# Layer 3 on one core: one run of local attention over all four images, with the other images' norms, projections and experts as steps beside it

## The chip, the core and the metric

One core of one Trainium2 chip runs the whole program in one launch. The metric is device microseconds of one execution, the median of the runs of a measurement; lower is better. The engines of the core that the profile names are PE (matmul; its weight loads are PEld), DVE (vector), ACT (scalar), POOL (GpSimd) and SP, whose queue issues every DMA of the part that is changed.

## What is computed

The program is a chain of four hybrid layers over a batch of 4 images of 64x64 tokens with 128 channels, all in float32. Layers 0 to 2 (a selective scan, a gated recurrence, an attention and a sparse expert layer) are not touched and are left out here. Layer 3 takes the tokens `t` (4 images x 4096 tokens x 128) and computes a local attention and then a mixture of 8 experts, each on a layer norm and each added back:

```python
t = t + _L3_attn_ref(_ln_t(t), ...)
t = t + _L3_ffn_ref(_ln_t(t), ...)

# _L3_attn_ref
xb = x @ w_down.T + b_down                      # 128 -> 16 channels
win = transpose(xb[:, idx, :])                  # windows of 144 tokens, every 72
q, k, v = split(win.reshape(-1, 144, 16) @ in_proj_w.T + in_proj_b, 3)
attn = softmax(q @ k.T / 2)                     # 4 heads of 4 channels, 144 x 144 a window
o = (attn @ v) @ out_proj_w.T + out_proj_b
att = overlap_add(o) / counts
out = x + sigmoid(gate) * (att @ w_up.T + b_up)
return layer_norm(out) * ln_gamma + ln_beta

# _L3_ffn_ref
router_probs = softmax(x @ router_w + router_b)         # 8 experts
top_p, top_i = top_k(router_probs, 2); top_p /= top_p.sum(-1)
expert_out = einsum('bnd,edc->bnec', x, expert_w) + expert_b
return einsum('bnk,bnkc->bnc', top_p, take(expert_out, top_i))
```

An image has 56 windows. Four of them are worked on together, one on each group of 32 rows of the PE, so an image is 14 "turns" of the attention (`NM` = 14).

## The kernel before

`layer3` works image by image. `windows(b)` and `chosen(b)` are Python generators: each `yield` gives the word back to the loop that drives them, and what stands between two yields is a step. The order of PE's instructions is exactly the order in which the steps are recorded (`manual_schedule(engines={PE})`); the order of the other engines and of SP's queue is decided by the framework when the program is built, by data and buffers, and is then fixed too. Every engine takes its instructions in that order, so an instruction that waits holds up all behind it on its engine.

`windows(b)` has these parts. They are named here as the text uses them.

- **Norms and down-projection** ("front"). All 8 blocks of 512 tokens are loaded into one tile `t` that stays for the whole image. A block is normalised (`cm.layer_norm`, L135 to L142: statistics on DVE, a square root on ACT, a reciprocal and four multiply-subtracts on DVE), transposed by PE (L103), copied out of PSUM by ACT (L105) and projected to 16 channels (L1727, sum with the bias L1731).
- **Projections.** The 16-channel tokens go to DRAM and come back as windows in `f` (the text's "wait for f"). Then, for 3 turns at a time, PE makes `kt` (L1771), the queries `qm` of four heads (L1775) and the values `vt` (L1785); ACT and DVE copy them out of the PSUM buffers `mm`, of which there are two.
- **Attention.** For each turn: `largest` (L1807: scores, reduced to row maxima by DVE, L1815) runs 4 turns ahead; `turned` (L1825) transposes the maxima and sends them through DRAM into `qm`; `weights` (L1847: scores again, exponentials on ACT, L1854), `values` (L1870, into the PSUM tile `po`, copied by ACT, L1881) and `divided` (L1889; DVE L1894, L1895). Half a turn is two `weights`, two `values`, one `largest` and one `divided`. `largest` and `weights` each take both buffers of the PSUM pool `s`.
- **Recombination and up-projection** ("back"). The halves of the windows are added (`rec`), transposed (L1945), projected up (L1962), added to the tokens (DVE, L1967), normalised, scaled and shifted (three POOL instructions of 128x512 each, L1970 to L1976).

`chosen(b)` does the expert part of an image: a norm and transpose for each block (L103, L142), the router (L1989), softmax and the two best of 8 on DVE ("gating"), and then, for each block, a transposition of the gate weights (L2040), the bias of the experts (L2048), and for each 128 tokens two matmuls of four experts each (L2058), every one of which is followed by four DVE instructions (L2064) that add the four experts' outputs with their weights to the tokens. These 64 matmuls of an image are called "expert matmuls". Each writes the PSUM pool `x`, which has one buffer, so one matmul cannot begin until the four DVE instructions of the one before are done.

The loop that drives them makes one step of `chosen(b - 1)` at each yield of `windows(b)`, that is four a turn, and ends what is left before the next image:

```python
for b in range(B):
    for _ in windows(b):
        next(before, None)
    for _ in before:
        pass
    before = chosen(b)
for _ in before:
    pass
```

So image 0's attention stands alone, those of images 1 to 3 have the expert matmuls of the image before among them, norms, projections and recombination stand between the attentions, and the experts of image 3 stand alone at the end.

Of the kernel before, what the change touches and what calls it, by code (L numbers as in the profile page):

```python
# [14 lines left out]
P = 128  # L15
# [1588 lines left out]
def layer3(cm, W, M, cst, x2, out):  # L1604
# [6 lines left out]
    with ExitStack() as ctx:  # L1611
# [4 lines left out]
        tp = ctx.enter_context(tc.tile_pool(name="ct", bufs=2))  # L1616
        ep = ctx.enter_context(tc.tile_pool(name="ce", bufs=10))
# [75 lines left out]
        for i in range(2):  # L1693
            vp = tl(wp, [HALF, 2, G, NH, 32], f"vp{i}")
            nc.gpsimd.memset(vp, 0.0)
            vps.append(vp)

# [11 lines left out]
        def windows(b):  # L1709

            t = tl(tp, [P, NT, D], "t")
            kept[b] = t
            for k in range(NBLK):
                nc.sync.dma_start(
                    t[:, 4 * k : 4 * k + 4, :],
                    x2[b, k * BLK : (k + 1) * BLK, :].rearrange("(t p) c -> p t c", p=P),
                )
            xl = tl(bp, [P, NT, D], "xl")
            xb = tl(bp, [P, NT, DK], "xb")
            xb_d = tl(dr, [S, DK], "xb_d")  # L1720
            xTs = {}

            def down(k):
                xT = xTs.pop(k)
                ps = tl(pp, [P, 4, DK], "mm")
                for i in range(4):
                    nc.tensor.matmul(  # L1727
                        ps[:, i, :], lhsT=xT[:, i * P : (i + 1) * P], rhs=wdT,
                        start=True, stop=True,
                    )  # L1730
                nc.vector.tensor_tensor(  # L1731
                    xb[:, 4 * k : 4 * k + 4, :], ps,
                    bdn.unsqueeze(1).to_broadcast([P, 4, DK]), ALU.add,
                )

            for k in range(NBLK):
                part = xl[:, 4 * k : 4 * k + 4, :]
                cm.layer_norm(part, t[:, 4 * k : 4 * k + 4, :], p2)
                xT = tl(p2, [P, BLK], "xT")
                cm.transpose4(xT, part, pp, "mm", act=True)  # L1740
                xTs[k] = xT
                yield
                if k:
                    down(k - 1)
            down(NBLK - 1)
# [17 lines left out]
            qm = tl(bp, [P, NM, NH, WIN], "qm")  # L1763
            kt = tl(bp, [P, NM, WIN], "kt")
            vt = tl(bp, [HALF, NM, 2, G, NH, HD + 1], "vt")
            for m0 in range(0, NM, GW):
# [3 lines left out]
                ps = tl(pp, [P, GW, WIN], "mm")  # L1770
                nc.tensor.matmul(ps[:, 0:g], lhsT=wk4, rhs=f[:, ms, :], start=True, stop=True)  # L1771
                nc.scalar.copy(kt[:, ms, :], ps[:, 0:g])
                for h in range(NH):
                    ps = tl(pp, [P, GW, WIN], "mm")
                    nc.tensor.matmul(  # L1775
                        ps[:, 0:g], lhsT=wq4[:, h, :], rhs=fq, start=True, stop=True
                    )
                    if h % 2:
                        nc.scalar.copy(qm[:, ms, h, :], ps[:, 0:g])
                    else:  # L1780
                        nc.vector.tensor_copy(qm[:, ms, h, :], ps[:, 0:g])
                ps = tl(pp, [HALF, GW, 2, G * NH * (HD + 1)], "mm")
# [6 lines left out]
                nc.vector.tensor_copy(  # L1789
# [3 lines left out]
                yield  # L1793

            mxs = {}

            def largest(m, a):
                if m % 2 == 0 and a == 0:  # L1800
                    mxs[m // 2] = tl(p2, [QC, G, 2, 2 * QN], "mx")
                mx = mxs[m // 2]
                ss = [tl(sp, [P, 2, BLK], "s") for _ in range(2)]
                for r in range(QN):
                    for i in range(G):
                        rows = slice(32 * i, 32 * i + 32)
                        nc.tensor.matmul(  # L1807
                            ss[i // 2][0:QC, i % 2, r * WIN : (r + 1) * WIN],
                            lhsT=qm[rows, m, 2 * a : 2 * a + 2, :].rearrange(
                                "p h q -> p (h q)"  # L1810
                            )[:, r * QC : (r + 1) * QC],
                            rhs=kt[rows, m, :], start=True, stop=True,
                        )
                for p in range(2):
                    nc.vector.tensor_reduce(  # L1815
                        mx[:, 2 * p : 2 * p + 2, m % 2, a * QN : (a + 1) * QN],
                        ss[p][0:QC, :, 0 : QN * WIN].rearrange("p j (r k) -> p j r k", k=WIN),
                        AX.X, ALU.max, negate=True,
                    )

            def turned(m):
                mx = mxs.pop(m // 2)
                n = G * 2 * 2 * QN
                ps = tl(pp, [P, BLK], "mm")
                nc.tensor.transpose(  # L1825
                    ps[0:n, 0:QC], mx.rearrange("p i m x -> p (i m x)"), cm.ident[0:QC, 0:QC]
                )
                mT = tl(p2, [n, QC], "mT")
                nc.vector.tensor_copy(mT, ps[0:n, 0:QC])
                m_d = tl(dr, [G, 2 * NH * WIN], "m_d")  # L1830
                nc.sync.dma_start(m_d.rearrange("i (x q) -> (i x) q", q=QC), mT)
                for i in range(G):
                    nc.sync.dma_start(
                        qm[32 * i + DK : 32 * i + R, m - 1 : m + 1].rearrange(
                            "p m h q -> p (m h q)"
                        ),
                        m_d[i : i + 1, :],
                    )

            o = tl(bp, [HALF, NM, G, 2, DK], "o")  # L1840
            es, oxs = {}, {}

            def weights(m, c, a):
                ss = [tl(sp, [P, 2, BLK], "s") for _ in range(2)]
                for i in range(G):
                    rows = slice(32 * i, 32 * i + 32)
                    nc.tensor.matmul(  # L1847
                        ss[i // 2][0:HALF, i % 2, 0 : 2 * WIN],
                        lhsT=kt[rows, m, c * HALF : (c + 1) * HALF],
                        rhs=qm[rows, m, 2 * a : 2 * a + 2, :], start=True, stop=True,  # L1850
                    )
                for p in range(2):
                    e = tl(ep, [HALF, 2, 2, WIN], "e")
                    nc.scalar.activation(  # L1854
                        e.rearrange("p j h q -> p j (h q)"), ss[p][0:HALF, :, 0 : 2 * WIN],
                        AF.Exp, scale=0.5,
                    )
                    es[m, p, c, a] = e

            def values(m, i):  # L1860
                p, j = divmod(i, 2)
                vp = vps[m % 2]
                if i == 0:
                    nc.gpsimd.tensor_copy(  # L1864
                        vp[:, :, :, :, 0 : HD + 1].rearrange("p c i h d -> p (c i h) d"),
                        vt[:, m].rearrange("p c i h d -> p (c i h) d"),
                    )
                for c in range(2):
                    for h in range(NH):
                        nc.tensor.matmul(  # L1870
                            po[32 * h : 32 * h + 32, j, :],
                            lhsT=vp[:, c, i, h, :], rhs=es[m, p, c, h // 2][:, j, h % 2, :],
                            start=(c == 0), stop=(c == 1),
                        )
                if j == 0:
                    return
                for c in range(2):
                    for a in range(2):
                        del es[m, p, c, a]
                ox = tl(p2, [P, 2, WIN], "ox")  # L1880
                nc.scalar.copy(ox, po)  # L1881
                oxs[m, p] = ox

            def divided(m, p):
                ox = oxs.pop((m, p))
                pt = tl(pp, [P, 4, NH, 32], "mm")
                for j in range(2):
                    for c in range(2):
                        nc.tensor.transpose(  # L1889
                            pt[0:HALF, 2 * j + c].rearrange("p h d -> p (h d)"),  # L1890
                            ox[:, j, c * HALF : (c + 1) * HALF], cm.ident,
                        )
                rc = tl(p2, [HALF, 4, NH], "rc")
                nc.vector.reciprocal(rc, pt[0:HALF, :, :, HD])  # L1894
                nc.vector.tensor_tensor(  # L1895
                    o[:, m, 2 * p : 2 * p + 2].rearrange("p j c (h d) -> p (j c) h d", d=HD),
                    pt[0:HALF, :, :, 0:HD],
                    rc.unsqueeze(3).to_broadcast([HALF, 4, NH, HD]), ALU.mult,
                )

            AHEAD = 4
            for m in range(-AHEAD, NM + 2):
                for x in range(4):
                    if 0 < m <= NM:
# [269 lines left out]
```

## Time and profile before

| | us |
|---|---|
| time before, median of 3 runs | 11145.42 (11142.15 to 11153.18) |
| the profiled execution, time | 11161.64 |
| its span, first to last instruction | 11159.9 |
| last matmul of layer 2 ends, at | 9152.9 |
| first `largest` of images 0, 1, 2, 3, at | 9267.2, 9692.8, 10120.5, 10551.6 |
| last `divided` of image 3 ends, at | 10806.6 |

Of the span, layers 0 to 2 take the first 9153 us and layer 3 the last 2007. Busy shares over the whole span are PE 85%, DVE 69%, POOL 49% and ACT 47%, but they mix the layers: POOL works almost only in layer 0. The profile's rows name engine, line, operation, output and inputs; PEclk is the clock that the throttle granted to PE, 1.00 being full speed. A float32 matmul of this kernel shows as two records, so "x2" on a row of one matmul is one matmul.

### The profile page before, as it was taken

The page shows a single profiled execution, that of the slowest core. Times are in us where ns is not written, and L with a number is a line of the kernel's source. Part 1 is how long each engine was busy: PE and PEld are TensorE (multiplying, and loading weights), DVE is VectorE, ACT ScalarE, POOL GpSimd, SP SyncE. Part 2 cuts the span into 40 slices and gives each one's busy share as a digit, 9 for nine tenths or more (in the row PEclk, how much of TensorE's full clock was granted, in tenths as well). Part 3 has the DMA queues.
Part 4 walks back from the last instruction along what each step waited for, and adds up shares of the span by engine and source line. Part 5 has one row for each costly group of instructions (what it writes and reads, how often), then busy time and mean ns, then how long its engine had stood idle before and what let it go on. Part 6 is the DMA issues. An engine that isn't in the chain of part 4 may idle for free. (4 is left out here: it accounts for less than half of the span.)

```text
span 11159.9 us, 163057 instructions
## 1 busy us (share of the span) xinstructions
PE 9472.5 (85%) x59368; PEld 4541.5 (41%) x59368; DVE 7705.4 (69%) x11365; ACT 5228.1 (47%) x13128; POOL 5468.6 (49%) x2661
## 2 busy tenths in 40 slices
PE   6889998889998899988899946999999858678685
PEld 2344443344443344443344423444444344344442
DVE  1899998888998888888899965635450132565563
ACT  6666544555445564445542124767776512132230
POOL 0778888878888888888899920000000000110110
PEclk7899999889998899998899968999999965688785
DMA  5334443334443334433333241111100180000100
GB/s 145 107 104 151 138 125 118 112 106 154 137 125 124 115 119 148 135 123 116 104 111 100 92 128 37 39 30 41 33 22 16 54 221 5 6 15 10 15 8 8
DMA packets 1378486, 975.88 MB, mean 87 GB/s; under 512 B 694980, under 2 KB 1195432, under 8 KB 1373336
## 3 DMA queue, kind: packets, MB, share of 16 engines
q1 hardware_dynamic: 1377688, 965.45, 28.9%
q8 instruction: 475, 7.78, 0.3%
q14 instruction: 323, 2.65, 0.1%
HBM read 650.24 MB, written 314.83 MB: 86 GB/s over the span
## 5 line engine op out<-in xcount | busy, mean ns | idle before, releaser
L657 DVE TENSOR_TENSOR_SCAN big<-dA,db 128x1024 f32<-128x1024 f32 x2048 | 4679.7, 2286 | 81.1 <-ACT dA L564 2.8
L673 POOL TENSOR_TENSOR big<-big,ct 128x2048 f32<-128x2048 f32 x1024 | 4645.5, 4537 | 84.7 <-DVE big L657 5.7
L641 PE MATMUL db<-dg,du 64*64 64x512 f32 x16384 | 2449.2, 619 | 100.5 <-DVE db L654 87.6
L686 PE MATMUL aux<-big,both 128*64 128x256 f32 x16384 | 2116.1, 402 | 465.2 <-DVE db L654 258.4
L686 PEld LDWEIGHTS aux<-big,both 128*64 128x64 f32 x16384 | 1205.0, 142 | 1462.9 <-issue 628.0
L705 ACT COPY yr<-aux 128x64 f32<-128x64 f32 x1024 | 226.6, 222 | 2759.4 <-PE aux L686 1295.4
L641 PEld LDWEIGHTS db<-dg,du 64*64 64x64 f32 x16384 | 747.3, 136 | 1328.7 <-issue 1224.6
L612 ACT ACTIVATE dg<-mask,BT 128x64 f32<-128x64 f32 x4096 | 1007.3, 341 | 4.4 <-DMA dg_d<-dg 4.4
L1443 PE MATMUL av<-e,x 128*128 128x512 f32 x2048 | 974.0, 592 | 4.6 <-ACT e L1438 4.6
L1394 PE MATMUL qk<-a,xT 128*128 128x512 f32 x2048 | 966.6, 594 | 8.6 <-ACT e L1398 7.8
L1398 ACT ACTIVATE e<-qk,nk 128x512 f32<-128x512 f32 x1024 | 692.9, 685 | 540.1 <-PE qk L1394 539.2
L564 ACT ACTIVATE dA<-dp,A 128x252 f32<-128x252 f32 x2048 | 870.7, 509 | 1.4
L973 POOL TENSOR_TENSOR g_rs<-g_rs,qrow 128x4 f32<-128x4 f32 x32 | 41.1, 1285 | 1500.4 <-DVE g_rs L972 1500.4
L1864 POOL COPY vp<-vt 72x160 f32<-72x160 f32 x56 | 18.9, 343 | 1470.8 <-PE po L1870 1074.9
L665 POOL TENSOR_TENSOR cy<-big,a 128x32 f32<-128x32 f32 x1008 | 269.3, 267 | 764.2 <-DVE big L657 483.8
L1394 PEld LDWEIGHTS qk<-a,xT 128*128 128x128 f32 x2048 | 378.0, 190 | 462.4 <-issue 358.0
L2064 DVE SCALAR_TENSOR_TENSOR t<-x,gw,t 128x128 f32<-128x128 f32 x1024 | 354.1, 346 | 301.5 <-PE x L2058 278.4
L1443 PEld LDWEIGHTS av<-e,x 128*128 128x128 f32 x2048 | 381.6, 190 | 434.7 <-issue 393.7
L1438 ACT ACTIVATE e<-e 128x1024 f32<-128x1024 f32 x510 | 538.7, 1056 | 15.3
L654 DVE TENSOR_TENSOR db<-db,cy 128x16 f32<-128x16 f32 x2016 | 336.5, 167 | 268.8 <-PE db L641 220.2
L2058 PE MATMUL x<-ew,x3T 128*128 128x512 f32 x512 | 365.0, 802 | 158.6 <-DVE t L2064 153.6
L1854 ACT ACTIVATE e<-s 72x576 f32<-72x576 f32 x448 | 269.3, 642 | 475.9 <-PE s L1847 475.4
(491 smaller groups left out, 10720.8 us busy)
## 6 DMA issues: line engine op xcount, KB each, us to landing
ct<-ct_d SPq DMA_DIRECT2D x1024, 128.0 KB
dg_d<-dg SPq DMA_DIRECT2D x256, 512.0 KB
dg<-dg_d SPq DMA_DIRECT2D x256, 512.0 KB
xo<-xT_d SPq DMA_DIRECT2D x2048, 32.0 KB
x<-xc_d SPq DMA_DIRECT2D x144, 264.0 KB
dp<-dl_d SPq DMA_DIRECT2D x256, 128.0 KB
t2k<-in_x SPq DMA_DIRECT2D x96, 256.0 KB
sp<-sp_d SPq DMA_DIRECT2D x16, 1280.0 KB
```

The lines of the kernel that those rows point to most:

```text
L564: nc.scalar.activation(w["dA"][:, :, g, n, 1:], w["dp"][:, g, :, 1:], AF.Exp, scale=A[:, w["h"], g, n : n + 1],)
L612: nc.scalar.activation(q["dg"][:, n, :], mask, AF.Copy, scale=BT[:, q["c"], n : n + 1])
L641: nc.tensor.matmul(bs[j][p * TC : (p + 1) * TC, g * NH0 : (g + 1) * NH0, :], lhsT=q["du"][kp][half, g * TC : (g + 1) * TC], rhs=q["dg"][ha ...
L657: nc.vector.tensor_tensor_scan(st[:, u].rearrange("p n t -> p (n t)"), q["w"]["dA"][:, c % QC].rearrange("p g n t -> p (g n t)"), bs[j].re ...
L673: nc.gpsimd.tensor_tensor(sv, sv, q["ct"].rearrange("p n t -> p (n t)").unsqueeze(1) .to_broadcast([P, 4, NH0 * TC]), ALU.mult,)
L686: nc.tensor.matmul(yp[p * TC : (p + 1) * TC], lhsT=both, rhs=st[:, :, p * NH0 + n, :], start=(n == 0), stop=(n == NH0 - 1 and not late),)
L1394: nc.tensor.matmul(ps, lhsT=me["xT"][:, kt * P : (kt + 1) * P], rhs=me["a"][k], start=True, stop=True,)
L1398: nc.scalar.activation(e[:, j, :], ps, AF.Exp, bias=me["nk"][:, kt : kt + 1], scale=2.0)
L1438: nc.scalar.activation(es[g + 2], es[g + 2], AF.Exp)
L1443: nc.tensor.matmul(avs[b, k], lhsT=img[b]["x"][:, kt, :], rhs=e[:, j, :], start=(kt == 0), stop=(kt == NT - 1),)
L2058: nc.tensor.matmul(s.rearrange("p e c -> p (e c)"), lhsT=x3T[:, j * P : (j + 1) * P], rhs=ew[:, 4 * a : 4 * a + 4, :].rearrange("p e c -> ...
L2064: nc.vector.scalar_tensor_tensor(t[:, j, :], s[:, e, :], gw[:, j, 4 * a + e : 4 * a + e + 1], t[:, j, :], ALU.mult, ALU.add,)
```

## The change

Layer 3 is rewritten around one loop over all 56 turns of the four images.

- `largest`, `turned`, `weights`, `values` and `divided` count turns `T` from 0 to 55 through all images. There are two sets of `qm`, `kt` and `vt` (a pool `qp` of two buffers), so the maxima of an image's first turns can be made while the image before is still in its last ones.
- `windows` is split: `front(b)` (norms, down-projection, projections), `merged(b)` (the additions of `rec`) and `back(b)` (recombination, up-projection, norm). `front(0)` runs first, alone. The others are put on a list `todo` with `chosen(b)`, and `step()` does the next step of the first entry. The loop calls `step()` 13 times in half a turn (6 times in an even quarter, 7 in an odd one).
- Beside image 0's attention stands `front(1)`; from the end of image b on, beside the attention of image b+1, stand `back(b)`, then `front(b + 2)`, then `chosen(b)`. After the last turn come `back(3)` and `chosen(3)`, alone.
- Matmuls of the steps beside the attention write the one buffer of the pool `x` (`own_bank`): transposes, projections, router, biases and experts alike. Where nothing runs beside (`front(0)`, `back(3)`, `chosen(3)`), they use the two buffers of `s` (`free_bank`).
- Tokens are kept in DRAM, not in a tile: blocks of 512 tokens come in two buffers `tin`; the normalised ones (`xl`) and the attention's result (`t`) are written to DRAM and loaded again. `chosen` does an image in two halves of 4 blocks and loads its tokens twice.
- A norm takes its root on POOL (a power of -0.5 on 128x4), and the scaling is done by four ACT instructions instead of four on DVE. The three POOL instructions of 128x512 in `back` go to DVE; the copies of `qm` and `vt` that DVE made go to ACT.

A step count for each part follows from the yields: `back` 56, `front` 125 (49 for the norms, 16 empty ones for the way through DRAM, 60 for the projections), `chosen` 228 (two halves of 24 for the norms, 10 for the gating and 80 for the experts). The 14 turns of an image have 364.

```diff
+        qp = ctx.enter_context(tc.tile_pool(name="cq", bufs=2))
...
+        mroot = tl(wp, [P, 1], "mroot")
+        nc.vector.memset(mroot, -0.5)
...
+        def own_bank():
+            return tl(xp, [P, BLK], "x")
+
+        def free_bank():
+            return tl(sp, [P, 2, BLK], "s")[:, 0, :]
+
+        def block(a, b, k, tag="tin"):
+            t = tl(tp, [P, 4, D], tag)
+            nc.sync.dma_start(t, rows(a, b, k))
+            return t
...
+            nc.vector.tensor_scalar(rs[:, 0, :], mv[:, :, 1], 1e-5, None, ALU.add)
+            nc.gpsimd.tensor_tensor(
+                rs[:, 0, :], rs[:, 0, :], mroot.to_broadcast([P, 4]), ALU.pow
+            )
+            nc.vector.scalar_tensor_tensor(
+                rs[:, 1, :], mv[:, :, 0], -1.0, rs[:, 0, :], ALU.mult, ALU.mult
+            )
...
+        def normalise(dst, src, rs):
+            for i in range(4):
+                nc.scalar.activation(
+                    dst[:, i, :], src[:, i, :], AF.Identity,
+                    bias=rs[:, 1, i : i + 1], scale=rs[:, 0, i : i + 1],
+                )
...
+                ps = bank()
+                turned4(ps, xl)
+                xT = tl(p2, [P, BLK], "xT")
+                nc.scalar.copy(xT, ps)
+                yield
+                yield
+                ps = bank()[:, 0 : 4 * DK].rearrange("p (i d) -> p i d", d=DK)
...
-                nc.gpsimd.tensor_tensor(
-                    dst, dst, gam.unsqueeze(1).to_broadcast([P, 4, D]), ALU.mult
-                )
...
+                nc.vector.tensor_tensor(
+                    xl, xl, gam.unsqueeze(1).to_broadcast([P, 4, D]), ALU.mult
+                )
+                nc.vector.tensor_tensor(t, t, bet.unsqueeze(1).to_broadcast([P, 4, D]), ALU.add)
+                yield
+                nc.vector.tensor_tensor(t, t, xl, ALU.add)
+                nc.sync.dma_start(rows(me["t"], 0, k), t)
...
-                        s = tl(xp, [P, 4, D], "x")
+                        s = bank()
                         nc.tensor.matmul(
...
                         yield
+                        yield
...
+            for _ in front(0, free_bank):
+                pass
+            fronts = {1: front(1, own_bank)}
+            todo.append(fronts[1])
+            for T in range(-AHEAD, LAST + 2):
+                b, m = divmod(T + AHEAD, NM)
+                if m == 0 and 0 < b < B:
+                    while fronts[b] in todo:
+                        step()
+                for x in range(4):
+                    if 0 < T <= LAST:
+                        values(T - 1, x)
+                    step()
+                    if x % 2 == 0 and T + AHEAD < LAST:
+                        largest(T + AHEAD, x // 2)
+                    if x == 2 and T % 2 == 0 and 1 < T + AHEAD <= LAST:
+                        turned(T + AHEAD - 1)
+                    step()
+                    step()
+                    if x == 2 and 0 < T <= LAST:
+                        divided(T - 1, 0)
+                    step()
+                    if x == 0 and 1 < T:
+                        divided(T - 2, 1)
+                        b, m = divmod(T - 1, NM)
+                        if m == 0:
+                            merged(b - 1)
+                            todo.append(back(b - 1, own_bank if b < B else free_bank))
+                            if b + 1 < B:
+                                fronts[b + 1] = front(b + 1, own_bank)
+                                todo.append(fronts[b + 1])
+                            if b < B:
+                                todo.append(chosen(b - 1, own_bank))
+                    step()
+                    if 0 <= T < LAST:
+                        weights(T, x // 2, x % 2)
+                    step()
+                    if x % 2:
+                        step()
+            while todo:
+                step()
+            for _ in chosen(B - 1, free_bank):
+                pass
```

## The prediction

> **What bounds the kernel now.** I read the busy time in stretches cut at the first `largest` of each image, then finer stretches for the granted clock, then the timeline of PE and DVE inside two stretches. Layers 0 to 2 are the same before and after; all that follows is on the last 2007 us.
>
> ```profile
> core 0: us, PE busy (x) PEld busy (x) DVE busy (x) ACT busy (x) POOL busy (x), PEclk, DMA share, GB/s
> 9153.00:9267.00 114.00, 59.48 (x204) 33.93 (x205) 31.90 (x136) 16.53 (x34) 0.61 (x2) 0.64 0.36 65
> 9267.00:9514.00 247.00, 231.79 (x2140) 118.57 (x2139) 71.52 (x129) 80.50 (x142) 4.10 (x12) 0.54 0.01 2
> 9514.00:9693.00 179.00, 103.74 (x442) 73.17 (x444) 98.71 (x477) 31.53 (x70) 30.91 (x26) 0.61 0.10 5
> 9693.00:10120.00 427.00, 321.85 (x2777) 180.84 (x2774) 251.13 (x859) 111.43 (x217) 35.03 (x38) 0.81 0.08 13
> 10120.00:10552.00 432.00, 330.01 (x2791) 184.92 (x2793) 252.18 (x861) 111.51 (x217) 35.05 (x38) 0.79 0.08 13
> 10552.00:10806.00 254.00, 224.67 (x2333) 109.83 (x2325) 152.67 (x383) 79.66 (x147) 4.13 (x12) 0.93 0.04 11
> 10806.00:11160.00 354.00, 197.15 (x444) 88.34 (x444) 164.79 (x605) 21.36 (x46) 30.30 (x24) 0.50 0.02 6
> ```
>
> In order: front of image 0; its attention alone; its back and the front of image 1; two periods of an image; image 3's attention with image 2's experts; the rest of image 3. No engine is full over a period (DVE 59%), and image 0's attention is bound by PE, 94% busy, at a clock of 0.54. Finer stretches show that busy time does not buy the clock:
>
> ```profile
> 9380.00:9420.00 40.00, 38.79 (x383) 20.03 (x381) 12.46 (x22) 14.36 (x25) 0.68 (x2) 0.60 0.01 2
> 9820.00:9860.00 40.00, 38.29 (x427) 19.39 (x425) 25.87 (x63) 14.30 (x26) 0.69 (x2) 1.00 0.03 9
> ```
>
> The first is attention alone, the second has an expert matmul in every quarter turn. Alone, half a turn takes 8.46 us, from one `largest` to the next:
>
> ```profile
> 9344.67 1.77 PE L1807 MATMUL s<-kt,qm 32*96 32x144 f32 x24
> ...
> 9353.13 1.98 PE L1807 MATMUL s<-kt,qm 32*96 32x144 f32 x24
> ```
>
> The expert matmuls of image 3, alone at the end, show the chain through the one buffer `x`: matmul 2.05, four DVE adds 1.51, handovers 0.18, together 3.74 us each. PE stands 1.69 us of it:
>
> ```profile
> 11003.26 2.05 PE L2058 MATMUL x<-ew,x3T 128*128 128x512 f32 x2 [1.69 <-DVE t L2064]
> 11005.35 1.51 DVE L2064 SCALAR_TENSOR_TENSOR t<-x,gw,t 128x128 f32<-128x128 f32 x4 [2.23 <-PE x L2058]
> 11007.00 2.04 PE L2058 MATMUL x<-ew,x3T 128*128 128x512 f32 x2 [1.70 <-DVE t L2064]
> ```
>
> Among `largest`, whose reductions take DVE 2.02 us in one go, a link is stretched again:
>
> ```profile
> 9701.26 1.35 PE L2058 MATMUL x<-ew,x3T 128*128 128x512 f32 x2
> ...
> 9701.30 2.02 DVE L1815 TENSOR_REDUCE mx<-s 96x6 f32<-96x864 f32 x2 [0.19 <-PE s L1807]
> ...
> 9703.24 1.49 DVE L2064 SCALAR_TENSOR_TENSOR t<-x,gw,t 128x128 f32<-128x128 f32 x4
> ...
> 9704.88 1.75 PE L2058 MATMUL x<-ew,x3T 128*128 128x512 f32 x2 [2.27 <-DVE t L2064]
> ```
>
> From 9694.59 to 9759.34 there are 18 such links, 3.6 us each, at a clock of about 0.77 with PE 70% busy.
>
> **The change part by part.** I cost four stretches of the new order.
>
> *A, the front of image 0.* It ran 114 us. Its eight blocks were loaded at once and normalised every 3.6 us. Now a block waits for one of two `tin` buffers: load, statistics 1.25 (0.87 + 0.36), root, scaling, load again. The root on POOL has a nearest row of the same shape:
>
> ```profile
> L973 POOL TENSOR_TENSOR g_rs<-g_rs,qrow x32: 1006/1007/1954, 6926.7 to 8889.5; 128x4 f32<-128x4 f32 x32
> ```
>
> so 1.01 to 1.95, against 0.30 + 0.16 for root and reciprocal. In the built order of DVE the instruction that needs the root mostly comes directly behind the one that feeds it, so DVE waits too, and statistics of later blocks and `largest` reductions queue behind. Estimate 5 us a block: +11, A = 124. (The missing table loads of ACT, 1.28 us a switch, are under 12 us in all and inside these roundings.)
>
> *B, image 0's attention, 247 before.* Beside the first turns stands front(1): 8 blocks x 5 = 40; the wait for f, 15 to 17 us in the trace, 15 here because one `largest` fills it; projections of five groups through the single buffer, each a chain of six matmuls (0.9, four of 1.5, 1.0) and six copies on ACT (about 0.5, handover 0.2, often behind an exponential of 0.64), 12 to 14 a group, 64. The built order leaves 26.5 half turns with nothing beside them: 26.5 x 8.46 = 224. B = 343. What front(1) costs here, 96 us, leaves the stretch behind 9514.
>
> [...] (Warm rows at 9786 to 9790: `weights` 0.72, `values` 0.70, `largest` 1.15, `divided` 0.60, so 4.6 a half turn against 8.46.)
>
> *C, beside the attention of images 1 to 3.* 13 steps stand in half a turn, and the chain of image b has 409 of them (56 + 125 + 228), 284 without a front. 409 + 409 + 284 = 1102 against 3 x 364 = 1092: the list stays full to the last turn, so C is as long as its steps take.
>
> Experts: 160 steps hold 64 matmuls, 6.5 in half a turn where there were two, all through `x`. PE meets the next one after a few of its own 0.6 to 1.2 us pieces, long before DVE is done, and being in order holds the attention up. A link is matmul + 1.70. Warm 2.76, cold 3.75; at the clock of the links above I take a matmul of 1.45, so 64 x 3.15 = 202. Gate transposes and biases now use `x` too: 0.6 + 0.58 + 1.1 + 0.68 and handovers, 3.6 x 8 = 29. Each half turn also puts reductions and divisions (2.0 + 0.47 on DVE) into the chain, most of it outside a running matmul: 12.3 x 1.6 = 20. Together 251, warm 220, cold 290.
>
> The rest, 249 steps or 19.2 half turns: attention alone takes 162. The parts alone took, in the trace: recombination 9 and up-projections with their norms 40 (10806 to 10855), 16 blocks of the two norms 57 (9566 to 9623), wait for f 17, projections 37, gating 12.1, counted twice for the two halves: 184. If all were hidden, 184; if nothing, 346. I take 270, near the middle: the cover is there (PE has attention to do), but single buffers of `x` and pairs of `tin` and `xl` set a latency for each block, and DVE takes three additions of at most 0.69 us (L1597) a block from POOL. Against that the four scalings (0.34 on DVE each, up to 1.42 beside POOL's additions) go to ACT, where the nearest row is 0.34 for 128x64 (L612), about 1.5 a block; ACT is busy 26% of a period.
>
> An image is 251 + 270 = 521; the last, without front, 251 + 142 = 393 (9.6 half turns 81, parts 102, same rule). C = 521 + 521 + 393 = 1435. The copies given from DVE to ACT are inside.
>
> *D, image 3's end.* 354 before. Two buffers now: recombination 9, up-projections 50 (the 40 before and 1.3 a block for root and reload), norms 46 (8 x 5 and a first load of 6), gating 24. Expert matmuls are set by DVE at 1.51 if PE warms, by PE at 2.05 if not: 1.6, so 64 x 1.6 + 8 x 2.7 = 124. D = 253, 101 saved.
>
> *Cost nothing:* DMA. Blocks go 64 times an image instead of 16, 256 KB each; DMA engines were busy 8% in a period. SP's queue now has block loads that wait for buffers ahead of the stores and loads of the maxima; these are made four turns ahead and have about two turns (over 30 us) in hand. Without that cover each would cost PE its trip, for which SP's waits show 3.0 us at most.
>
> **Sum.** 124 + 343 + 1435 + 253 = 2155 against 2007: +148. On the profiled time of 11161.64 that is 11310; that execution is 16.2 us over the median of the runs, so on the median 11293.
>
> **Rivals.**
>
> *Faster: the overlap holds.* Expert matmuls in every half turn keep the clock at 1.00 as in 9820 to 9860, links run at 2.76 and most of the rest is hidden: 225 + 200 an image, 330 the last, C = 1180, total -107: 11040. For it: that stretch, PE 96% busy. Against it: that stretch has two matmuls a half turn, and where links touch each other (11020 to 11060, PE 60% busy) the clock is 0.50. It decides when C is under 1287, that is, an image under about 470.
>
> *Slower still: orders lock.* Nothing of the rest is hidden, since DVE waits for POOL's root, ACT's scalings wait behind that, exponentials behind them, and PE behind these: 346 an image and experts 265; C = 611 x 2 + 448 = 1670, +383: 11530. For it: static orders, POOL, DVE, ACT and PE in one chain for every block. Against it: 8.46 us of PE work stand in each half turn to fill the holes.
>
> *Nothing:* gains at the end (101) and losses in the middle cancel within 0.2%, 22 us, which is what a measurement of this kernel can tell from no change.
>
> **How the numbers follow.** Forecast 0.62, faster 0.14, locked 0.20, nothing 0.04. The locked case is slower too: slower 0.82. The range: experts 220 to 290 and the rest 184 to 346 in three images, A, B and D by about 35 each, do not all fall to one end; from the forecast I reach down to a small loss of time that leaves half of the faster case out, 11110, and up to 11480, which leaves about half of the locked case out.
>
> **What would show it.** Right: image 0's recombination begins near 9620 instead of 9514, and the images beside which steps stand take over 480 each; waits of PE for DVE L2148 (expert adds) of over 100 us; clock in expert stretches 0.65 to 0.85; image 0's later turns at 8.4 to 8.5 a half turn; the last experts at 1.5 to 1.8 each. Wrong: expert stretches with half turns under 18 us, or the attention of image 0 at a clock near 1.00.

## The result and the profile after

The changed kernel takes 11342.52 us (median of 4 runs, 11334.17 to 11350.89) against 11149.3 for the kernel before (4 runs beside it, 11142.15 to 11155.65): ratio 1.0173, 95% interval 1.0156 to 1.0191. It is slower by 193 us, where +148 was forecast, and the time lies inside the range. The profiled execution is the fastest of the four, 11334.17; its span is 172.5 us longer than that of before.

The busy time in stretches, cut at the ends of the forecast's A, B, C and D, and within the first image of C also where the expert matmuls begin and end (columns as before: length, busy time of each engine, granted clock, DMA):

```profile
core 0: us, PE busy (x) PEld busy (x) DVE busy (x) ACT busy (x) POOL busy (x), PEclk, DMA share, GB/s
9153.00:9278.00 125.00, 62.82 (x207) 34.49 (x209) 20.29 (x133) 36.86 (x80) 12.69 (x14) 0.63 0.38 60
9278.00:9626.00 348.00, 300.27 (x2649) 157.90 (x2648) 99.09 (x201) 115.27 (x212) 8.82 (x18) 0.64 0.10 15
9626.00:9880.00 254.00, 209.78 (x1649) 120.63 (x1647) 96.99 (x382) 105.41 (x220) 23.11 (x28) 0.62 0.23 50
9880.00:10005.00 125.00, 91.47 (x547) 37.48 (x546) 60.88 (x173) 19.32 (x37) 3.04 (x5) 0.70 0.05 16
10005.00:10044.00 39.00, 31.40 (x277) 19.31 (x276) 18.80 (x106) 15.05 (x31) 2.71 (x4) 0.63 0.13 37
10044.00:10168.00 124.00, 90.37 (x566) 37.73 (x564) 63.32 (x169) 17.97 (x33) 1.03 (x3) 0.72 0.05 14
10168.00:10700.00 532.00, 428.10 (x3058) 219.07 (x3058) 240.04 (x827) 157.47 (x320) 29.46 (x39) 0.67 0.15 34
10700.00:11087.00 387.00, 272.64 (x1726) 133.14 (x1727) 178.76 (x667) 92.73 (x190) 19.73 (x25) 0.66 0.12 34
11087.00:11333.00 246.00, 135.62 (x442) 71.09 (x440) 147.05 (x593) 41.02 (x93) 17.05 (x16) 0.72 0.17 50
```

Rows one and two are A and B. The first is cut at 9153, where layer 2 of the kernel before ends; in this run layer 2 ended at 9147.5, so A is 130 us and not 125. Rows three to six are the 542 us beside image 1's attention: 254 for back, front(2) and the first norms and gating, 125 for half the experts, 39 for the second norms and gating, 124 for the other half. Then come 532, 387 and the end. In the expert rows PE is busy 73% at a clock of 0.70 to 0.72, and DVE 50%: no engine is full. The chain of waits over layer 3 (who waited for whom, us in total, times, longest) says why:

```profile
engine line waited for: us in total, times, longest us
...
DVE tin L2148 <- PE x L2142: 286.0, 166, 3.4
...
PE x L2142 <- DVE tin L2148: 175.9, 145, 2.4
...
DVE ln_rs L1739 <- POOL ln_rs L1736: 101.9, 95, 1.5
```

PE waits 176 us for the adds of the experts, the adds wait 286 us for PE: two engines taking turns through one buffer. One link beside the attention, in the timeline:

```profile
9904.43 2.08 PE L2142 MATMUL x<-ew,x3T 128*128 128x512 f32 x2
9904.54 2.02 DVE L1873 TENSOR_REDUCE mx<-s 96x6 f32<-96x864 f32 x2 [1.31 <-PE s L1865]
9906.55 1.51 DVE L2148 SCALAR_TENSOR_TENSOR tin<-x,gw,tin 128x128 f32<-128x128 f32 x4
9908.20 2.04 PE L2142 MATMUL x<-ew,x3T 128*128 128x512 f32 x2 [1.70 <-DVE tin L2148]
```

It is the link that the kernel before had alone at its end: 3.77 us here, 3.74 there. Attention matmuls that could run stand in PE's order behind the one that waits. At the end, with two buffers, the same matmuls come in pairs:

```profile
11189.92 2.13 PE L2142 MATMUL s<-ew,x3T 128*128 128x512 f32 x4 [0.80 <-DVE tin L2148]
...
11191.06 2.67 DVE L2148 SCALAR_TENSOR_TENSOR tin<-s,gw,tin 128x128 f32<-128x128 f32 x8 [0.25 <-PE s L2142]
...
11192.84 2.13 PE L2142 MATMUL s<-ew,x3T 128*128 128x512 f32 x4 [0.80 <-DVE tin L2148]
```

A pair comes every 2.92 us, so 1.46 us each where one took 3.74: DVE (2.67 of 2.92) sets the pace.

### The profile page after: what moved, and what is told of

Same layout as the page of the kernel before. It is cut to its first block, busy times and chain, and to the rows that moved or that the text cites. A ratio compares the mean times of both kernels' runs of the same rounds, so it can differ in the third digit from the quotient of the medians.

```text
span 11332.4 us, 163576 instructions
## 1 busy us (share of the span) xinstructions
PE 9623.2 (85%) x59368; PEld 4580.7 (40%) x59368; DVE 7600.0 (67%) x11174; ACT 5376.2 (47%) x13471; POOL 5445.0 (48%) x2661
## 5 line engine op out<-in xcount | busy, mean ns | idle before, releaser
L1736 POOL TENSOR_TENSOR ln_rs<-ln_rs,mroot 128x4 f32<-128x4 f32 x96 | 98.7, 1028 | 926.7 <-DVE ln_rs L1735 866.2
L1873 DVE TENSOR_REDUCE mx<-s 96x6 f32<-96x864 f32 x224 | 226.3, 1048 | 434.8 <-PE s L1865 434.6
```

The lines of the kernel that those rows point to most:

```text
L1873: nc.vector.tensor_reduce(mx[:, 2 * p : 2 * p + 2, m % 2, a * QN : (a + 1) * QN], ss[p][0:QC, :, 0 : QN * WIN].rearrange("p j (r k) -> p j ...
```

## The experiments

Each kernel is compared with the kernel before, run beside it on the same chip. Stage lengths are read in one profiled run of each, cut at the first `largest` and at the first recombination transpose of each image (D: from image 3's to the end). In the text, C is the sum of images 0 to 2, and A is read from the end of layer 2 of the same run. Layers 0 to 2 are the same in every kernel here, but end anywhere from 9131 to 9164 us in the profiles, so up to 33 us between two profiled runs is not of layer 3:

| us | B | image 0 | image 1 | image 2 | D |
|---|---|---|---|---|---|
| changed kernel | 349 | 542 | 533 | 387 | 244 |
| e2_two_x | 347 | 442 | 414 | 273 | 244 |
| e3_one_add | 355 | 467 | 445 | 289 | 242 |
| e4_no_root | 353 | 531 | 522 | 402 | 234 |
| e5_mixed | 356 | 400 | 384 | 309 | 238 |
| e7_mixed_filler | 373 | 397 | 402 | 319 | 236 |
| e9_less_pe | 337 | 527 | 529 | 384 | 244 |
| e10_less_act | 357 | 527 | 526 | 398 | 237 |

**The end alone** (kernel before, one edit):

```diff
-                        s = tl(xp, [P, 4, D], "x")
+                        if b == B - 1:
+                            s = tl(sp, [P, 2, BLK], "s")[:, 0, :].rearrange(
+                                "p (e c) -> p e c", c=D
+                            )
+                        else:
+                            s = tl(xp, [P, 4, D], "x")
```

> The kernel before, with one edit: the expert matmuls of image 3, which stand alone at the end, write the two buffers of the pool s in place of the one buffer x; nothing else moves. In the profile of before these 64 links take about 252 us (10902 to 11154, 3.74 us each plus the gates). Theory (the one buffer makes the chain, and the end is a gain that needs nothing else of the change): a link falls to what DVE alone needs, 1.5 to 1.85 us, as the end of the changed kernel shows (two halves of 59.5 and 61 us): the end falls by about 125 us and the whole to about 11024. Rival (the clock): with PE not full the clock stays near 0.50, matmuls at 2.05 us bound the link, and the gain is 252 - (64 x 2.2 + 22) = 90 us: about 11060. If the gain of the end came from something else in the change (tokens by blocks, halves), the time does not move.

Measured 11001.75 against 11155.92, ratio 0.9853 (0.9812 to 0.9895). In its profile the first and the last expert matmul of image 3 stand 109 us apart, where it was 250 (10904 to 11154). The timeline shows the same pair as above:

```profile
10942.26 2.13 PE L2063 MATMUL s<-ew,x3T 128*128 128x512 f32 x4 [0.80 <-DVE t L2069]
...
10943.40 2.67 DVE L2069 SCALAR_TENSOR_TENSOR t<-s,gw,t 128x128 f32<-128x128 f32 x8 [0.25 <-PE s L2063]
...
10945.18 1.10 PE L2063 MATMUL s<-ew,x3T 128*128 128x512 f32 x2 [0.80 <-DVE t L2069]
```

So the second buffer alone brings more than all that the change gained in D (354 to 244), and needs nothing else of the change. PE's matmuls are shorter too: two records take 1.10 where they took 2.05. The clock of these matmuls rose with it, against the rival. Before, and in this run:

```profile
10903.00:11154.00 251.00, 151.15 (x218) 48.97 (x216) 93.86 (x260) 4.02 (x7) 0.00 (x0) 0.50 0.03 8
10905.00:11016.00 111.00, 80.82 (x217) 30.09 (x215) 88.21 (x261) 4.02 (x7) 0.00 (x0) 0.98 0.06 17
```

**A second buffer beside the attention** (changed kernel):

```diff
-        pp = ctx.enter_context(tc.tile_pool(name="cp", bufs=2, space=PSUM))
+        pp = ctx.enter_context(tc.tile_pool(name="cp", bufs=1, space=PSUM))
-        xp = ctx.enter_context(tc.tile_pool(name="cx", bufs=1, space=PSUM))
+        xp = ctx.enter_context(tc.tile_pool(name="cx", bufs=2, space=PSUM))
```

> The changed kernel, with one PSUM buffer moved: the pool x has two buffers, the pool mm one. All else is as changed. Theory (what costs beside the attention is the chain matmul, four adds, next matmul through one buffer, and the same between transposes, copies and projections): PE's waits for the expert adds (176 us in the profile of the changed kernel) go mostly away. PE was busy 75% of the 249 us of an image's experts, 187 us, so these stretches fall to about 195 and C by about 150, and the front and back of an image, which take turns through x too, give some 15 an image more: about 11140 to 11180. Rival (fixed orders and DVE: the adds come in bursts between largest reductions, and PE meets the next matmul too soon even with two buffers): C falls by less than 60, 11290 or more; and with one buffer mm the divisions can wait for each other, a loss of up to 20.

Measured 10992.48 against 11155.92, ratio 0.985 (0.9811 to 0.989): one buffer moved turns the loss into a gain. The three images take 1129 us instead of 1461, about 332 less. Image 0 in its stretches, cut as above:

```profile
9620.00:9867.00 247.00, 207.83 (x1652) 123.22 (x1651) 97.75 (x382) 105.56 (x220) 22.93 (x28) 0.62 0.25 51
9867.00:9945.00 78.00, 70.77 (x569) 31.56 (x572) 59.72 (x176) 19.64 (x37) 3.05 (x5) 0.89 0.09 25
9945.00:9984.00 39.00, 31.83 (x263) 20.61 (x257) 18.04 (x104) 14.75 (x31) 2.67 (x4) 0.59 0.13 36
9984.00:10062.00 78.00, 69.40 (x562) 31.78 (x560) 59.16 (x164) 17.99 (x33) 1.03 (x3) 0.90 0.08 22
```

The expert halves fall from 125 and 124 to 78 and 78, and everything else stays (254 to 247, 39 to 39). The wait that the theory named goes from 175.9 us to:

```profile
PE x L2142 <- DVE tin L2148: 24.3, 36, 2.1
```

C fell by nearly twice what was expected (150 for the experts and some 15 an image for front and back), because the expectation took PE's busy time in the expert stretches as given. It was not: it fell from 91 to 71 us for a half, as the clock went from 0.70 to 0.89. Of the 47 us that a half lost, about 26 are idle time of PE that is gone, and about 21 are shorter matmuls. Fewer waits on PE went with a faster PE; no run here separates the two.

**Fewer adds, one buffer** (changed kernel; the adds for three of the four experts of each matmul of images 0 to 2 are left out):

```diff
-                        for e in range(4):
+                        for e in range(4 if bank is free_bank else 1):
```

> The changed kernel with three of the four DVE additions behind every expert matmul of images 0 to 2 left out (the other three experts of each matmul are left out of these images' results); image 3 is whole. x keeps its one buffer. Theory (the chain through x): a link loses three additions of 0.38 us, 1.13 us, 64 times an image in three images: -217, to about 11125; PE's waits for these adds fall from 176 us to below 40. Rival (PE and its clock bound the stretch, and the waits stand for time that PE would need anyway): PE's busy time of 187 us an image is the floor, and at a clock that stays at 0.6 to 0.8 the gain is 30 us an image or less, 11250 or more.

Measured 11065.38 against 11155.92, ratio 0.992 (0.9898 to 0.9941), 277 us under the changed kernel where the chain gave 217. PE's waits for these adds fall from 175.9 to 44.8 us, where under 40 was expected. C falls by 261, and the clock in the expert stretches is up to 0.82 and 0.94 (stretches of the profile):

```profile
9906.00:9996.00 90.00, 77.74 (x572) 34.43 (x565) 30.99 (x81) 19.05 (x37) 3.05 (x5) 0.82 0.08 22
10038.00:10117.00 79.00, 68.31 (x566) 30.88 (x566) 31.08 (x73) 17.99 (x33) 1.04 (x3) 0.94 0.08 22
```

A shorter chain (this run) and a chain of the same work in two buffers (the run before) bring nearly the same, and the second does so with all of DVE's work in place. So the expert stretch was held by the handover through one buffer, not by how much DVE or PE had to do.

**No root on POOL** (changed kernel):

```diff
-            nc.gpsimd.tensor_tensor(rs[:, 0, :], rs[:, 0, :], mroot.to_broadcast([P, 4]), ALU.pow)
+            nc.vector.reciprocal(rs[:, 0, :], rs[:, 0, :])
```

> The changed kernel with the root of each of the 96 block norms taken off POOL: a DVE reciprocal of 128x4 stands in its place, so the square root itself is left out of the results (all the rest has its size and order). In the profile of the changed kernel POOL takes 1.03 us for a root, and DVE waits 102 us for them in all, 1.07 each. Theory (the root is on the path of every block, as the forecast has it in A, C and D): 0.9 to 1.1 us a block, -85 to -105 in all, about 11245; of this about 8 in A, 8 in D and 75 in C. Rival (DVE's wait is covered, since PE has attention to do beside it and DVE is busy under half): A and D gain 1 a block, about 16 to 24 with the last image's, C nothing: 11320.

Measured 11309.42 against 11155.92, ratio 1.0131 (1.0086 to 1.0177). In its profile D gains 11 us and A 4; image 0 and 1 are 11 shorter each, image 2 is 15 longer, B 4 longer. In C as a whole that is 7 us of 1461, where the theory asked for 75: near the rival's case. The time alone hardly tells: its interval, 11252 to 11353 us, holds the rival's 11320 and ends 7 us from the theory's 11245. In C, most of DVE's 102 us of waiting for the root stood under other work.

**Front and experts side by side** (on top of e2_two_x):

```diff
+        def both(gs):
+            while gs:
+                for g in list(gs):
+                    if next(g, gs) is gs:
+                        gs.remove(g)
+                    else:
+                        yield
...
-                                fronts[b + 1] = front(b + 1, own_bank)
-                                todo.append(fronts[b + 1])
...
-                                todo.append(chosen(b - 1, own_bank))
+                                nxt = [front(b + 1, own_bank)] if b + 1 < B else []
+                                todo.append(both(nxt + [chosen(b - 1, own_bank)]))
```

> The changed kernel with two buffers x and one mm (as in e2_two_x), and one more edit: front(b + 2) and chosen(b) stand on the list side by side, a step of one and a step of the other in turn, in place of one after the other; chosen has its own two tin buffers. The number of steps and of all instructions is the same. In e2_two_x the stretches of image 0 were: back 70 us at a clock of 0.50, norms of front 79 at 0.50, projections 59 at 0.95, norms and gating 38 and 37 at about 0.58, experts 79 and 77 at 0.90. Theory (the clock: wherever a 128-row matmul of the experts stands in every quarter turn the clock is 0.9 or more, and norms among them ride on it): norms and projections (138) and chosen (231), 369 together, fall to about 310 in images 0 and 1, so C falls by about 110 to 1020 and the whole to about 10880. Rival (PE needs the same time anyway, or the chain of a norm's block holds the expert matmuls up): C stays within 30, 10960 to 11020. A half turn's steps bring half as many experts, so DVE is spread better in both cases.

Measured 10944.85 against 11135.44, ratio 0.9827 (0.9808 to 0.9846), the lowest of all that was run; its interval overlaps those of e1_end_pairs and e2_two_x. C falls by 36 us in the profile where 110 was expected: images 0 and 1 give 42 and 30, but image 2, which has no front to mix in, takes 36 back, and its last 21 us have no expert matmuls left beside them. The projections now stand among expert matmuls at a clock of 0.92 to 0.98; back and the norms remain at 0.50 to 0.57 for 145 us of images 0 and 1.

**A filler for the clock** (kernel before; the same matmul was then put into two other kernels):

```diff
+                    if b == 0 and 0 <= m < NM:
+                        nc.tensor.matmul(
+                            tl(xp, [P, 4, D], "x")[:, 0, :], lhsT=ew[:, 0, :],
+                            rhs=ew[:, 1, :], start=True, stop=True,
+                        )
                     yield
```

> The kernel before with one addition: in each quarter turn of image 0's attention, where nothing stands beside, PE makes one extra matmul of 128 rows, 128x128 by 128 columns, into x, which nobody reads. Nothing else moves. Theory A (128-row matmuls in a steady row buy the clock, as 9820 to 9860 of the kernel before seems to show: clock 1.00, 4.6 us of attention a half turn): the clock of the 247 us of image 0's attention rises from 0.54 to over 0.8, a half turn falls from 8.46 to about 6.5 with two fillers of 0.15 to 0.3, and the stretch falls by about 50 us: 11100. Theory B (the clock follows something else, such as how densely matmul columns follow each other on all rows): the clock stays near 0.5 and the two fillers cost 0.3 to 0.6 a half turn, +8 to +17 us: 11165 to 11175.

Measured 11114.05 against 11135.44, ratio 0.9981 (0.9967 to 0.9994). Image 0's attention took 204 us at a clock of 0.87, as theory A said, but the whole fell by 21 us, not by the 50 that theory A asked for: this stretch differs from run to run in the kernel before as well (the last section has its lengths).

> The kernel before with both small edits, of e1_end_pairs (image 3's expert matmuls in two buffers of s) and of e6_filler (a filler matmul in each quarter turn of image 0's attention). If the two gains stand side by side, -135 at the end (252 to about 115) and -43 in image 0's attention (247 to 204): about 10965. If the filler's gain is only the scatter of the clock from run to run (image 0's attention took 229 us at 0.64 in e1_end_pairs without any filler, 247 at 0.54 in the kernel before), the attention is at 204 us here only by chance, and the time is that of e1_end_pairs within 10 us.

Measured 10988.65 against 11147.64, ratio 0.9855 (0.9837 to 0.9873), against 0.9853 for the end alone. The stretch is again 204 us, so the length came twice, yet the whole is not measurably shorter than e1_end_pairs.

In the kernel of e5_mixed, the loop over turns got it too (`heavy` is set while a generator is among its expert matmuls):

```diff
+                    if 0 <= T < LAST and not heavy:
+                        nc.tensor.matmul(own_bank()[:, 0:D], lhsT=ew[:, 0, :], rhs=ew[:, 1, :],
+                            start=True, stop=True)
                     if 0 < T <= LAST:
                         values(T - 1, x)
```

> The kernel of e5_mixed with the filler of e6_filler (one matmul of 128 rows, 128x128 by 128 columns, into x, read by nobody) in every quarter turn in which no expert matmuls stand: image 0's attention, and the stretches of back, norms and gating of all images. Theory (the time beside the attention that two buffers did not win back is PE at a low clock, not waits for norms): in e5_mixed image 0's attention ran at 0.50 to 0.58 for most of 356 us, and back and norms at 0.50 to 0.57 for 145 us in images 0 and 1, with 60 more at 0.60 to 0.66. At the pace of e6_filler (204 where 247 was) the 216 us that stand alone in image 0 fall by 38, and 205 us in each of two images by 35, the last by some 20: -128, to about 10815. Rival (a block's chain DVE, POOL, ACT, PE sets the pace of back and norms, 10 us a block whatever PE's clock): only image 0's lonely turns gain, -38, and fillers cost 0.3 each where they bring nothing: 10900 to 10920.

Measured 11026.15 against 11147.64, ratio 0.99 (0.9879 to 0.9921): 80 us slower than e5_mixed, against both theories. The granted clock of image 0's lonely turns, with the filler in every quarter turn, in e8_end_and_filler:

```profile
9360.00:9440.00 80.00, 73.85 (x969) 41.46 (x969) 30.43 (x54) 34.03 (x60) 2.05 (x6) 1.00 0.01 3
```

and in e7_mixed_filler:

```profile
9500.00:9649.00 149.00, 139.50 (x1179) 73.79 (x1171) 37.61 (x72) 40.99 (x72) 2.40 (x7) 0.50 0.01 2
```

The matmuls are the same, and PE is busy 92% and 94%, but the granted clock is 1.00 over the 80 us of one and 0.50 over the 149 us of the other: half a turn takes 6.6 us there (13.17 a turn) and 9.9 to 11.1 here, two fillers included (0.80 us each here). The two kernels differ in more than the clock: the filler stands at another place in the quarter turn, and with one buffer `mm`, as in e2_two_x, PE waits 1.98 us for a copy of the maxima once in four half turns here. The half turns without that wait run at 0.50 as well. So the filler did not by itself bring a high clock here, and theory A does not hold in general, though the stretch was short both times in the kernel before (204 us at 0.87). What made the clock 1.00 in one run and 0.50 in the other is left open.

**What holds back, norms and gating?** Two cuts in the changed kernel, made to tell PE's own time from the way of a block through the engines. In e9_less_pe the four matmuls of a block's down-projection become one, and in the same way those of its router; in e10_less_act (the second diff) the four scalings of a norm become one:

```diff
-                for i in range(4):
+                if bank is own_bank:
                     nc.tensor.matmul(
-                        ps[:, i, :], lhsT=xT[:, i * P : (i + 1) * P], rhs=wdT,
-                        start=True, stop=True,
-                    )
+                        ps.rearrange("p i d -> p (i d)"), lhsT=xT[:, 0:P],
+                        rhs=xT[:, 0 : 4 * DK], start=True, stop=True,
+                    )
+                else:
...
```

```diff
-            for i in range(4):
-                nc.scalar.activation(
-                    dst[:, i, :], src[:, i, :], AF.Identity,
-                    bias=rs[:, 1, i : i + 1], scale=rs[:, 0, i : i + 1],
-                )
+            nc.scalar.activation(
+                dst, src, AF.Identity, bias=rs[:, 1, 0:1], scale=rs[:, 0, 0:1]
+            )
```

> The changed kernel (one buffer x), with PE's part of the steps in front and norms made smaller: the four down-projection matmuls of a block are one matmul of the same output size, and so are the four router matmuls, wherever they stand beside the attention (their results are left out; transposes, copies, sums and all the rest stay). A down-projection of a block takes PE 1.89 us at the low clock in these stretches (four matmuls with four weight loads), one takes about 0.5. Theory (back, norms and gating, 293 us an image, are PE's own time: attention at 8.46 a half turn and 2.95 a block added to it, PE busy 80% at a clock of 0.50 to 0.57): 1.4 off each of 16 blocks, 22 us an image in images 0 and 1, 11 in image 2, 11 in image 0's attention, -66 in all: about 1.011 of the kernel before. Rival (the way of a block through its engines sets the pace): each block is also 1.4 shorter, so this run alone could not tell; e10_less_act, in which the way is shorter by 1.0 and PE's work is the same, tells them apart. If both stay within 10 us, neither PE nor the way of a block is the bound.

Measured 11289.35 against 11140.61, ratio 1.0137 (1.012 to 1.0154).

> The changed kernel (one buffer x), with the four ACT scalings of every norm (128x128 each, 0.41 apart, 1.65 a block) made one ACT instruction of 128x512 with the first token group's scale and bias (those of the other three are left out). About 0.6 a block in place of 1.65, on the way of every block, and PE's work is the same. Theory (PE's own time at a low clock): C and B within 10 us; A and the norms of D, where PE waits for each block, 0.5 to 1 a block, 8 to 24 in all: about 1.016 of the kernel before. Rival (the way of a block through DVE, POOL, ACT and PE sets the pace): 1.0 off each of 24 blocks an image, -24 in images 0 and 1, -16 in image 2, -8 in image 0's attention, with A and D -85 to -95: about 1.009.

Measured 11287.8 against 11140.61, ratio 1.0131 (1.0114 to 1.0147). The changed kernel stands at 1.0173; both theories gave e9_less_pe 1.011, and it made a little over half of that. e10_less_act lies between what PE's own time (1.016) and the way of a block (1.009) gave it, and its interval holds neither. The stages lean to PE's own time: e9_less_pe is 12 shorter in B and 15 in image 0, while e10_less_act is 11 shorter over C and 8 longer in B. But one image's length moves by some 15 us for no reason in its work (image 2 is 15 longer in e4_no_root, with less to do), so this is not settled.

## Why the prediction was right, and which terms were off

The sign and the mechanism held. By its steps, forecast and profile: A 124 and 130; B 343 and 349; C 1435 and 1461; D 253 and 244. In the profile that is 178 us more in layer 3 than the 2007 before, where the sum gave 148.

*Experts, 251 an image.* 125 and 124 measured, 249. That the chain through `x` does it, the forecast could only argue from rows of the kernel before; e2_two_x and e3_one_add show it, by two different edits. The named signs came: PE's waits for L2148 are 176 us, the clock of these stretches is 0.70 to 0.72, and image 0's recombination begins at 9626. A link, from one expert matmul of a block to the next, takes 3.48 us on average in images 0 and 1, where 3.15 and 0.31 for reductions and divisions were put. Inside it two errors cancel: the matmul is 1.6 and not 1.45, the rest 1.9 and not 2.0. The clock that the 1.45 was put at was misread, too: from 9694.59 to 9759.34 of the kernel before it is 0.84, not about 0.77.

*The rest, 270 an image.* This is the term that was mis-sized: 254 + 39 = 293 in image 0. Its cause was wrong in part. The forecast blamed the latency of `x`, `tin`, `xl` and the root on POOL; a second `x` took 7 us of the 293 and no root 7 us of all C. The root itself was 1.01 in nearly all of the 96 norms, the low end of its bounds. PE is busy 83% of the 254 us at a clock of 0.62, so much of it may be PE's own time at that clock, but the last two experiments did not prove that.

*The last image, 393:* 387. *D:* the experts took 62 + 60 us, from the first gate transposition of a half to its last add, where 124 was put, and e1_end_pairs shows that the gain of the end stands by itself.

*B and the clock.* The lonely turns were put at 8.46 us half a turn, and most are 8.4 to 8.8, at a clock of 0.50. But from 9527 to 9607 they are 6.6 on average, at up to 1.00, with the same matmuls:

```profile
9460.00:9500.00 40.00, 39.57 (x348) 19.22 (x350) 11.84 (x21) 13.38 (x24) 0.68 (x2) 0.50 0.01 2
9580.00:9600.00 20.00, 18.07 (x257) 9.81 (x251) 7.37 (x13) 9.79 (x18) 0.52 (x2) 1.00 0.01 3
```

So the row was a good mean and not a constant; the kernel before itself has three half turns of 5.9 to 7.3 us from 9370 to 9391, its clock 1.00 from 9375 to 9387. (The rows that the forecast calls warm, 9786 to 9790, have a clock of 1.00.) The lonely turns took 219 instead of 224, the part beside front(1) 129 instead of 119.

*The faster rival* had the wrong condition. It asked whether the clock stays up among dense expert matmuls. In the expert stretches of image 0 the answer is no with one buffer (0.70 to 0.72) and mostly yes with two (0.89 to 0.90): its C was 1180, which the changed kernel did not come near, and e2_two_x, another kernel, has 1129. The forecast held that a high clock would make the chain short; the runs show that taking the chain's waits away (from 175.9 us to 24.3 in e2_two_x, to 44.8 in e3_one_add) came with a high clock (0.89 and 0.90, 0.82 and 0.94). The locked rival does not appear: C is 26 over the forecast and 209 under that rival's 1670. The rival *Nothing* was drawn too narrow: 22 us is not what a measurement can always tell here, for the kernel before, run beside e2_two_x, took 11108 to 11195.

## What to carry to other kernels

When work is moved beside other work on an engine that keeps a fixed order, count first the buffers through which the moved work hands over, and only then its busy time: with one buffer, PE stood 175.9 us here for the adds of the work beside the attention, and the attention with it; with two, 24.3. Look for the edit inside a large change that works alone: of this one, the second buffer at the end was worth 1.5% by itself. The same buffer beside the attention took back what the rest had lost, and no more that can be told: the whole rewrite with it stands at 0.985, the kernel before with the end alone at 0.9853, and only e5_mixed (0.9827) may be a little better. What two buffers `x` do in the kernel before, without the rewrite, beside the attentions of images 1 to 3, was not run. And take a stretch's busy time as a price only at the clock it was read at: half an image's experts kept PE busy for 91 us at 0.70 and for 71 at 0.89.

## What was not expected of the hardware

Read in windows of 4 us from 9267 to 9515, PE's granted clock in image 0's attention of the kernel before is 0.50 in 55 windows of 62, 1.00 in four, and 0.59 to 0.61 in three. In the lonely turns of the changed kernel, from 9406 to 9626, it is 0.50 in 36 windows of 55, 1.00 in 14, and between in five. The same attention and filler matmuls ran at 1.00 over 80 us of e8_end_and_filler, PE 92% busy, and at 0.50 over 149 us of e7_mixed_filler, PE 94% busy. Image 0's attention of the kernel before took 247 us at 0.54 in one run and 229 at 0.64 in another (e1_end_pairs, where nothing was changed there). The 149 us of e7_mixed_filler and the 40 us of the changed kernel from 9460 to 9500, 99% busy at 0.50, speak against busyness alone as the measure, and no run here shows what the measure is.

Waits of at most 2.4 us on PE, 175.9 us in all over images 0 to 2, stood beside a clock of 0.70 to 0.72 in the expert stretches of image 0, and a clock of 0.82 to 0.94 where two different edits had taken most of them away.
